# Layer 0's projected rows in DRAM: one copy of each part, repeated by the loads that read it

## The chip, the cores and the metric

The kernel runs on one core of one Trainium2 chip. A core has a tensor engine (PE, with its weight loads shown as PEld), a vector engine (DVE), a scalar engine (ACT), a general engine (POOL), a synchronisation engine (SP) that here only issues DMAs, and 16 DMA engines. The metric is the device time of one launch in microseconds. Three runs of the kernel before took 733.96, 735.86 and 736.60 us; the median, 735.86 us, is the time that is to be predicted anew. A change is told from no change here at about 0.5%, or 3.7 us.

## What is computed

Two transformer layers run over x of 8 batches x 256 tokens x 128 features. Each has a cross attention to a context of the same size, and a mixture of 8 experts of which every token uses two. The change touches only the attention of layer 0, which has 16 heads of width 8:

```python
q = _split_heads(query @ Wq.T + bq, B, Lq)
k = _split_heads(key @ Wk.T + bk, B, Lk)
scores = jnp.einsum('bhqd,bhkd->bhqk', q, k) / jnp.sqrt(jnp.float32(D_K))
mask = (hash_q[:, :, :, None] != hash_k[:, :, None, :]).astype(scores.dtype) * NEG
attn = jax.nn.softmax(scores + mask, axis=-1)
out = jnp.einsum('bhqk,bhkd->bhqd', attn, v)
```

## The kernel before

**Scores as one product of 74 or 77 rows.** A float32 product is had from bf16 matmuls: q and k are each cut into three bf16 parts whose sum is the float32 value, and all nine products of parts are summed by the tensor engine. So for each head both operands have 3 x 3 x 8 = 72 rows (`R_MASK`): for each of the nine pairs (i, j) and each of the 8 features d, the q operand `q9` holds part i of q and the k operand `k9` holds part j of k. The order of the 72 rows is free as long as both operands share it. Rows 72 and 73 carry the mask. Rows 74 to 76 (`R_MAX` to `R_ALL`) carry the negated row maxima, so that a second product gives score minus maximum, ready for the exponential.

**Stages.** The loop of layer 0 runs over n = 0 to 145. Step n is slot i = n % 16 of batch b = n // 16. In slot n the program has `scores` for slot n (line 533, two matmuls, then DVE's maximum on line 537), `probs` for the head of slot n - 15 (`LAG`; line 564, then ACT's exponential on line 571), and after every four heads `values0` (line 579). PE, ACT, DVE and SP run in the order in which the program was written out; SP's DMAs are therefore issued strictly one after another, and one that waits holds up those behind it.

**Side work.** Generators in the list `side` advance by one step in each slot, in the order in which they were appended. Two of them matter here:

- `prep0(b + 2)`, appended in slot i = 2 of batch b, makes q9 and k9 of batch b + 2, of which there are three buffers each. Counting its yields, its 14th and 15th steps (slots 15 of batch b and 0 of batch b + 1) issue the four mask rows (line 438), its 16th step falls into slot 1 of batch b + 1, and its 17th into slot 2. From step 16 on it writes the parts to a DRAM tile and loads them back: in steps 16 to 19 six writes (line 518), two, one, two and one to a step, and in step 20 the two reads (lines 521 and 522). `part` holds 128 partitions, which are (feature, head), by (part, q or k, token).
- `maxima(b, half)`, appended in slots 8 (half 0, heads 0 to 7) and 0 of the next batch (half 1, heads 8 to 15), has its third step in slots 10 and 2. That step transposes the maxima, copies them to `mT` (ACT, line 556) and issues one DMA of 12 KB on SP into rows 74 to 76 of q9 (line 557). The first `probs` that needs half 0 is in slot 15 of the batch, the first that needs half 1 in slot 7 of the next.

In slot 2 `prep0(b + 2)` stands before `maxima(b, 1)` in `side`, so its DMAs of that slot are ahead of that mT on SP's queue. Batch 0's operands are written without DRAM (`prep_first`). Batch 1's `prep0` is run to its end before the loop starts, with nothing between its steps.

**Other traffic.** POOL issues loads of later weights and inputs during batches 0 to 4, one in every second slot, and scatters rows to the experts during batches 5 to 7.

Of the kernel before, what the change touches and what calls it, by code (L numbers as in the profile page):

```python
# [12 lines left out]
BF16 = mybir.dt.bfloat16  # L13
# [6 lines left out]
S = 256  # L20
QT = S // P
D = 128
H = 16
DK0 = 8
# [27 lines left out]
NPART = 3  # L52
R_MASK = NPART * NPART * DK0
# [9 lines left out]
def kernel(  # L63
# [28 lines left out]
    nc = tc.nc  # L92
# [4 lines left out]
    dp = ctx.enter_context(tc.tile_pool(name="dp", bufs=3, space=bass.MemoryType.DRAM))  # L97
# [7 lines left out]
    def bank(tag, name, dt=F32):  # L105

        if tag == "any":
            third.append(third.pop(0))
            tag = third[-1]
        return ps.tile([P, 512 * 4 // mybir.dt.size(dt)], dt, tag=tag, name=name, bufs=1 if tag in ("pv", "y") else 2)  # L110
# [77 lines left out]
    with nc.allow_non_contiguous_dma(reason="two rows of biases, once"):  # L188
        for i, src in enumerate((bq0, bk0)):
            nc.scalar.dma_start(  # L190
                out=brow[:, i, :].rearrange("o (d g j) -> o d g j", d=DK0, g=4),
                in_=src.rearrange("(o j z) g -> o z g j", o=1, z=32)[:, :DK0],
# [190 lines left out]
    def norm_T(tiles, name, rows=None, lead=2):  # L383
        n = len(tiles)
        mv = sm.tile([P, GT, 2], F32, tag="mv", name=f"mv{name}", bufs=3)
        for i, t in enumerate(tiles):
            st = sm.tile([P, 6], F32, tag="bn", name=f"st{name}_{i}", bufs=3)
            nc.vector.bn_stats(out=st, in_=t)
            nc.vector.bn_aggr(out=mv[:, i, :], in_=st)
            if i == 1 and n > 2:  # L390
                yield
        ve = sm.tile([P, GT], F32, tag="ve", name=f"ve{name}", bufs=3)
        nc.vector.tensor_scalar(ve[:, :n], mv[:, :n, 1], EPS, None, ALU.add)
        rs = sm.tile([P, GT], F32, tag="rs", name=f"rs{name}", bufs=3)
        nc.gpsimd.tensor_tensor(rs[:, :n], ve[:, :n], mhalf[:, :n], ALU.pow)
        for _ in range(lead):
            yield
        xns = []
        for i, t in enumerate(tiles):
            if rows is None:  # L400
                xn = sm.tile([P, D], F32, tag="xn", name=f"xn{name}_{i}", bufs=4)
                to = xn
            else:
                xn = rows[:, i, 0, :D]
                to, t = rows[:, i, :, :D], t.unsqueeze(1).to_broadcast([P, 2, D])
            nc.vector.tensor_scalar(to, t, mv[:, i, 0:1], rs[:, i : i + 1], ALU.subtract, ALU.mult)
            xns.append(xn)
            if i == 1 and n > 2:
                yield
        for _ in range(1 if rows is None else 2):  # L410
            yield
        pt = bank("pt", f"np{name}")
        for i, xn in enumerate(xns):
            nc.tensor.transpose(pt[:, ts(i, P)], xn, ident)
        tag, bufs = (f"xnT{n}", 2) if rows is None else (f"xnTr{n}" if n == QT else f"xnT{n}", 1)
        xnT = wk.tile([P, n * P], F32, tag=tag, name=f"xnT{name}", bufs=bufs)
        nc.scalar.copy(xnT, pt[:, : n * P])
        yield
        return xnT
# [4 lines left out]
    def values(b):  # L424
        v = v0s[b % 4]
        pv = bank("pt", f"pvp0_{b}")
        for t in range(QT):
            nc.tensor.matmul(pv[:, ts(t, D)], lhsT=ct[b][:, ts(t, P)], rhs=wv0_sb, start=True, stop=True)
        nc.vector.tensor_tensor(
            v[:, :, :, :DK0],  # L430
            pv[:, : QT * D].rearrange("p (t h d) -> p t h d", t=QT, d=DK0),
            bv0_sb.rearrange("p (h d) -> p h d", d=DK0).unsqueeze(1).to_broadcast([P, QT, H, DK0]),
            ALU.add,
        )

    def mask_rows(b, t, k, engs):
        for i, eng in enumerate(engs):
            eng.dma_start(out=t[R_MASK + i : R_MASK + i + 1, :, :], in_=mrow[b * H : (b + 1) * H, k + i, :])
# [48 lines left out]
    def prep0(b):  # L487
        q9, k9, v = q9s[b % 3], k9s[b % 3], v0s[b % 4]
        xnT = yield from norm_T(xt[b * QT : (b + 1) * QT], f"a{b}", lead=6 if b >= 2 else 2)
        pq = bank("pt", f"pq0_{b}")  # L490
        nc.tensor.matmul(pq[:, :S], lhsT=wq0_sb, rhs=xnT, start=True, stop=True)
        nc.tensor.matmul(pq[:, S:], lhsT=wk0_sb, rhs=ct[b], start=True, stop=True)
        f = wk.tile([P, 2, S], F32, tag="g2", name=f"qk{b}", bufs=5)
        nc.scalar.activation(f[:, 0, :], pq[:, :S], AF.Identity, bias=bqk[:, 0:1], scale=1.0 / math.sqrt(DK0))
        nc.scalar.activation(f[:, 1, :], pq[:, S:], AF.Identity, bias=bqk[:, 1:2])
        yield

        part = wk.tile([P, NPART, 2, S], BF16, tag="pT", name=f"part{b}")
        rest = wk.tile([P, 2, S], F32, tag="g2", name=f"rest{b}", bufs=5)
        eng = nc.vector if b < 2 else nc.gpsimd  # L500
        eng.tensor_copy(part[:, 0], f)
        eng.tensor_tensor(rest, f, part[:, 0], ALU.subtract)
        eng.tensor_copy(part[:, 1], rest)
        eng.tensor_tensor(part[:, 2], rest, part[:, 1], ALU.subtract)
        yield
        values(b)
        yield
        for _ in range(2 if b >= 2 else 0):
            yield
        for t, k in ((q9, 0), (k9, 2)):  # L510
            mask_rows(b, t, k, (nc.sync, nc.sync))
            yield

        rows = dp.tile([2, R_MASK, H, S], BF16, tag="rows", name=f"rows{b}")
        for n, by in ((0, "(i j d) h s -> j (d h) i s"), (1, "(i j d) h s -> i (d h) j s")):
            to = rows[n].rearrange(by, i=NPART, j=NPART)
            for i in range(NPART):
                nc.sync.dma_start(out=to[i], in_=part[:, :, n, :])
                if b > 1 and i:
                    yield  # L520
        nc.sync.dma_start(out=q9[:R_MASK, :, :], in_=rows[0])
        nc.sync.dma_start(out=k9[:R_MASK, :, :], in_=rows[1])
        yield

    def scores(b, i):
# [579 lines left out]
    for _ in prep_first():  # L1105
        pass
    side.append(prep0(1))
    drain()
    for i in range(3):
# [4 lines left out]
    for n in range(NS * B + LAG + 3):  # L1114
        b, i = divmod(n, NS)
        if n < NS * B:
            scores(b, i)
        if 0 <= n - LAG < H * B:
            probs(*divmod(n - LAG, H))
        g, r = divmod(n - LAG - 5, 4)  # L1120
        if r == 0 and 0 <= g < 4 * B:
            values0(*divmod(g, 4))
            if g % 2:
                side.append(finish0(g // 4, g % 4 // 2))
        if i in (HH, 0) and HH <= n <= NS * B:
            side.append(maxima((n - 1) // NS, 1 if i == 0 else 0))
        if i == 2 and b + 2 < B:
            side.append(prep0(b + 2))
        if i == 6 and b in (3, 5, 7):
            one_by_one(route(0, 2 * (b - 3), GT, nc.gpsimd))  # L1130
            if b == 7:
                one_by_one(place(0, True))
                one_by_one(route(0, NT - 2 * QT, QT))
        if n == NS * B + 8:
            side.append(keys_values(0))
        tick()
        if n == NS * B + LAG - 2:
            begin0(range(4))
            tiles0 = run0()
        if n >= NS * B + LAG:  # L1140
            next(tiles0)
# [94 lines left out]
```

## Time and profile before

| | before |
|---|---|
| median of 3 runs | 735.86 us (733.96 to 736.60) |
| the profiled execution | 758.97 us, span 757.1 us |
| PE / DVE / ACT / POOL busy | 83% / 63% / 44% / 43% |
| mean granted PE clock | 0.927 of full speed |
| layer 0's attention in it | about 21 us (first `scores`) to 229 us (last `probs`) |
| DMA writes to the DRAM tile, line 518 | 42 of 192 KB, six for each of batches 1 to 7 |
| DMA reads of it, lines 521 and 522 | 7 + 7 of 576 KB |

The profile is of one execution, which took 3.1% longer than the median run. Its times are microseconds from the start of the span. A row of the timeline gives start, duration, engine and line, and in brackets how long the engine had been idle and what ended the idle time. An engine name with a q ("SPq") means the sequencer, which issues or waits; "[3.27 <-DMA x]" is a wait of 3.27 us that a DMA ended. "PEclk" is the share of full speed that the tensor engine's clock was granted.

### The profile page before, as it was taken

Reading aid. Unit: us, or ns where it says so; the run is one execution under the profiler, and the core shown is the slowest. Engines: PE = TensorE matmul, PEld = TensorE weight load, DVE = VectorE, ACT = ScalarE, POOL = GpSimd, SP = SyncE. Lnnn points to the kernel's source line nnn. Section 1 sums busy time; section 2 is a strip of 40 time slices with the busy share of each in tenths; the row PEclk is TensorE's granted clock in tenths of the full one; section 3 lists DMA queues with packets and bytes.
Section 4 is the critical chain, followed back from the end, with each engine's and each line's share of the span. In section 5 each row is a group of like instructions: output and inputs, shape, how many; then the busy total and the mean of one; then the engine's idle time right before and its main releaser. Section 6 shows DMA issues by size and latency. Waiting matters only on the chain.

```text
span 757.1 us, 15220 instructions
## 1 busy us (share of the span) xinstructions
PE 630.0 (83%) x4781; PEld 485.1 (64%) x4781; DVE 479.4 (63%) x1808; ACT 332.1 (44%) x1028; POOL 328.5 (43%) x398
## 2 busy tenths in 40 slices
PE   3699787768867779999999999999999784989990
PEld 2355454434435769986677777777777563879990
DVE  5778787666725455555777787877868772544442
ACT  1146554445522112235766565656556641423330
POOL 4445368260240544444433363535363551354442
PEclk9999998787768899999999999999999997999995
DMA  5577666650035446634020300000000015758845
GB/s 142 150 202 229 185 182 164 173 149 24 2 126 152 134 127 185 189 113 116 15 66 27 91 15 15 15 16 15 1 16 8 8 60 193 208 155 229 233 124 173
DMA packets 72318, 83.85 MB, mean 111 GB/s; under 512 B 9768, under 2 KB 55104, under 8 KB 71232
## 3 DMA queue, kind: packets, MB, share of 16 engines
q1 hardware_dynamic: 63640, 63.71, 30.2%
q0 software_dynamic: 7840, 18.97, 8.3%
q8 instruction: 39, 0.64, 0.4%
q14 instruction: 39, 0.32, 0.1%
q10 hardware_dynamic: 760, 0.21, 0.1%
HBM read 60.86 MB, written 30.60 MB: 121 GB/s over the span
## 4 chain that ended last, share of the span: by engine, by line
PE 27%; DVE 10%; issue 5%; ACT 4%; DMA 4%; POOL 4%; SPq 0%; POOLq 0%; ACTq 0%; DVEq 0%
PE s L962 4%; PE y L1037 4%; PE pt L1011 3%; PE o L1026 3%; POOL ys L860 3%; DVE ns L977 3%; PE pk L925 3%; ACT p L988 2%; PE pq L925 2%; DMA yy<-ys 2%; PE ph L830 2%; DVE pT L1013 2%; PE y L853 2%; DVE k L928 2%; PE pu L833 2%
## 5 line engine op out<-in xcount | busy, mean ns | idle before, releaser
L988 ACT ACTIVATE p<-ns,nm 128x256 f32<-128x256 f32 (+1 forms) x256 | 113.8, 447 | 33.9 <-DVE nm L977 29.2
L1001 POOL TENSOR_TENSOR p<-p,rd 128x1024 f32<-128x1024 f32 (+1 forms) x63 | 92.1, 1481 | 63.8 <-DVE rd L996 62.6
L860 POOL DMA_INDIRECT ys<-yj,xj x78 | 75.1, 963 | 89.5 <-DVE yj L858 78.3
L537 DVE TENSOR_REDUCE mx<-sc 128x2 f32<-128x512 f32 x128 | 83.8, 683 | 32.6 <-PE sc L533 25.2
L571 ACT ACTIVATE pT<-st 128x512 f32<-128x512 f32 x128 | 74.0, 596 | 64.2 <-PE st L564 60.7
L699 POOL DMA_INDIRECT xs<-rows,ati x64 | 63.0, 985 | 89.8 <-DVE rows L691 44.8
L977 DVE CUSTOM_DVE_ANT_0 ns<-s,tri 128x256 f32<-128x256 f32 (+1 forms) x256 | 77.0, 348 | 0.5 <-PE s L962 0.5
L1013 ACT COPY pT<-pt 128x512 f32<-128x512 f32 x64 | 36.8, 574 | 71.0 <-PE pt L1011 71.0
L564 PE MATMUL st<-q,k 77*128 77x256 bf16 x256 | 56.8, 310 | 13.2 <-DMA q<-mT 8.4
L533 PE MATMUL sc<-k,q 74*128 74x256 bf16 x256 | 57.2, 313 | 12.6 <-DVE mx L537 10.5
L1011 PE MATMUL pt<-ident,p 128*128 128x128 f32 x384 | 57.6, 278 | 4.9 <-POOL p L1001 3.2
L1011 PEld LDWEIGHTS pt<-ident,p 128*128 128x128 f32 x384 | 45.6, 142 | 24.3 <-DVE k L928 11.5
L1026 PE MATMUL o<-pT,v 128*64 128x256 f32 (+1 forms) x512 | 55.1, 339 | 4.9 <-ACT pT L1013 4.2
L839 DVE TENSOR_TENSOR h<-s,pu 128x256 f32<-128x256 f32 x78 | 24.0, 348 | 53.1 <-PE px L805 13.6
L823 ACT ACTIVATE h<-ph,wj 128x128 f32<-128x128 f32 x78 | 24.4, 364 | 72.7 <-issue 51.0
L820 PE MATMUL ph<-xT,wj 128*128 128x128 f32 x312 | 47.0, 296 | 9.9 <-DVE xT L807 5.7
L962 PE MATMUL s<-k,q 64*128 64x256 f32 (+1 forms) x512 | 53.2, 338 | 0.5 <-DVE nm L977 0.5
L1026 PEld LDWEIGHTS o<-pT,v 128*64 128x64 f32 x512 | 35.7, 138 | 23.7 <-ACT pT L1013 7.2
L962 PEld LDWEIGHTS s<-k,q 64*128 64x128 f32 x512 | 42.8, 186 | 10.3 <-issue 4.5
L988 ACT ACTIVATION_READ_ACCUMULATOR p<-ns,nm 128x1 f32 x256 | 48.6, 190 | 0.0
L820 PEld LDWEIGHTS ph<-xT,wj 128*128 128x128 f32 x312 | 40.2, 201 | 12.4 <-DVE xT L807 6.2
L533 PEld LDWEIGHTS <-q 74*128 74x128 bf16 x256 | 25.0, 109 | 35.9 <-issue 30.3
(227 smaller groups left out, 1290.5 us busy)
## 6 DMA issues: line engine op xcount, KB each, us to landing
wj<-wa SPq DMA_DIRECT2D x39, 352.0 KB
wj<-wa SPq DMA_DIRECT2D x39, 258.0 KB
rows<-part SPq DMA_DIRECT2D x42, 192.0 KB
xs<-blank SPq DMA_DIRECT2D x16, 325.0 KB
xj<-xs SPq DMA_DIRECT2D x78, 65.0 KB
yy<-ys SPq DMA_DIRECT2D x16, 256.0 KB
q<-rows SPq DMA_DIRECT2D x7, 576.0 KB
k<-rows SPq DMA_DIRECT2D x7, 576.0 KB
```

The costliest lines, as they stand in the source:

```text
L533: nc.tensor.matmul(sc[:, k, :], lhsT=q9s[b % 3][:R_MAX, h, ts(qt, P)], rhs=k9s[b % 3][:R_MAX, h, :], start=True, stop=True,)
L537: pace[0] = nc.vector.tensor_reduce(c0[b]["mx"][:, qt, 2 * u : 2 * u + 2], sc, AX.X, ALU.max)
L571: nc.scalar.activation(pT.rearrange("p t s -> p (t s)"), st, AF.Exp)
L699: nc.gpsimd.indirect_dma_start(out=xs[l][:, :], out_offset=to, in_=rows[:, i, k, :], in_offset=None),
L820: nc.tensor.matmul(phs[z][:, ts(i, P)], lhsT=wj[:, o : o + P], rhs=xT, start=True, stop=True)
L860: free(f"ys{l}", nc.gpsimd.indirect_dma_start(out=ys[l][:, :], out_offset=to, in_=yj, in_offset=None))
L962: nc.tensor.matmul(u["s"][a, r][:, (1 - qt) * S : (1 - qt) * S + n], lhsT=c1[b]["q"][rows, c, ts(qt, P)], rhs=c1[b]["k"][rows, c, :n], sta ...
L977: nc.vector.tensor_tensor_reduce(out=ns[:, o : o + n], in0=s[:, o : o + n], in1=tri[:, S - n :], scale=-1.0, scalar=3.0e38, op0=ALU.add, o ...
L988: nc.scalar.activation(p[:, o : o + n], ns[:, o : o + n], AF.Exp, bias=nm[:, a : a + 1], scale=-1.0, accum_out=u["sum"][:, 2 * i + a : 2 * ...
L1001: eng.tensor_tensor(p, p, rd[:, :, a : a + 1].to_broadcast([P, 4, n]), ALU.mult)
L1011: nc.tensor.transpose(pt[:, ts(n, P)], u["p"][:, i, (S, 0, P)[m] :][:, :P], ident)
L1026: nc.tensor.matmul(o[DK1 * r : DK1 * (r + 1), a, t * P :], lhsT=v[:, t, cols], rhs=pT, start=(t == 0), stop=True, skip_group_check=True,)
```

## The change

A part is written to DRAM once and not three times, and each read repeats a row three times. The 72 rows take a new order, r = 9d + 3i + j, the same that batch 0's operands have.

```diff
-        rows = dp.tile([2, R_MASK, H, S], BF16, tag="rows", name=f"rows{b}")
-        for n, by in ((0, "(i j d) h s -> j (d h) i s"), (1, "(i j d) h s -> i (d h) j s")):
-            to = rows[n].rearrange(by, i=NPART, j=NPART)
-            for i in range(NPART):
-                nc.sync.dma_start(out=to[i], in_=part[:, :, n, :])
-                if b > 1 and i:
-                    yield
-        nc.sync.dma_start(out=q9[:R_MASK, :, :], in_=rows[0])
-        nc.sync.dma_start(out=k9[:R_MASK, :, :], in_=rows[1])
+        rows = [dp.tile([R_MASK // NPART, H * S], BF16, tag=f"rows{n}", name=f"rows{b}_{n}") for n in range(2)]
+        to = rows[0].rearrange("(d i) (h s) -> i d h s", i=NPART, h=H)
+        for i in range(NPART):
+            nc.sync.dma_start(out=to[i], in_=part[:, i, 0, :])
+        nc.sync.dma_start(out=rows[1].rearrange("(j d) (h s) -> (d h) j s", j=NPART, h=H), in_=part[:, :, 1, :])
+        yield
+        src = rows[0].unsqueeze(1).to_broadcast([R_MASK // NPART, NPART, H * S])
+        nc.sync.dma_start(out=q9[:R_MASK, :, :], in_=src)
+        for j in range(NPART):
+            src = rows[1][ts(j, DK0), :].unsqueeze(1).to_broadcast([DK0, NPART, H * S])
+            nc.sync.dma_start(out=k9[j:R_MASK:NPART, :, :], in_=src)
         yield
```

The DRAM tile of q has 24 rows (d, i), that of k 24 rows (j, d), each of 8 KB. q's parts are written by three DMAs of 64 KB, k's by one of 192 KB. q9 is read by one DMA whose source has the counts 24, 3 and 4096; k9 by three whose sources have the counts 8, 3 and 4096, each into every third partition. The generator now writes in its 16th step, reads in its 17th, and is three steps shorter.

## Prediction

> **What bounds the kernel here.** I read the engine summary first, then the tensor engine's waits within layer 0's attention (20 to 230 us), then SP's and PE's timelines of one batch beside each other, then the windows around the waits.
>
> ```profile
> PE   3699787768867779999999999999999784989990
> PEclk9999998787768899999999999999999997999995
> ```
>
> PE is 60 to 90% busy through the attention, and its clock dips in some slices. It works in program order, so each wait of it moves the end. These are the waits:
>
> ```profile
> PE sc L533 <- DVE mx L537: 10.5, 16, 2.5
> PE st L564 <- DMA q<-mT: 8.4, 3, 4.3
> PE po L592 <- ACT oT L587: 8.3, 6, 6.6
> ...
> PE st L564 <- DMA k<-mrow: 3.3, 1, 3.3
> ```
>
> The reader should see that no large wait is for the row tile: q9 and k9 come in time (only 0.9 us, once). What PE waits for is mT, the 12 KB of maxima. SP's and PE's timelines of one batch show why:
>
> ```profile
> 59.47 1.21 SPq L438 DMA_DIRECT2D q<-mrow  x2
> 60.73 1.23 SPq L438 DMA_DIRECT2D k<-mrow  x2
> 62.00 1.98 SPq L518 DMA_DIRECT2D rows<-part  x3
> 64.63 0.79 SPq L557 DMA_DIRECT2D q<-mT  x1
> 65.46 1.57 SPq L518 DMA_DIRECT2D rows<-part  x3
> 67.28 0.36 SPq L521 DMA_DIRECT2D q<-rows  x1
> 69.79 0.31 SPq L522 DMA_DIRECT2D k<-rows  x1
> 73.61 0.77 SPq L557 DMA_DIRECT2D q<-mT  x1
> ```
>
> ```profile
> 67.92 0.39 PE L564 MATMUL st<-q,k 77*128 77x256 bf16 x2
> ...
> 76.43 0.38 PE L533 MATMUL sc<-k,q 74*128 74x256 bf16 x2 [0.23 <-DVE mx L537]
> 80.08 0.38 PE L564 MATMUL st<-q,k 77*128 77x256 bf16 x2 [3.27 <-DMA k<-mrow]
> ```
>
> The mT of 64.63 landed at 67.87 by the trace's semaphore records; the matmul at 67.92 is the first to need it. **It has no slack.** The mT of 73.61 was issued behind the two reads. It landed at 79.95, 6.3 us after its issue and 1.1 us after the read of k (78.86); later mTs with nothing beside them land in 2.0 us. The 3.27 us, which the view puts down to k<-mrow, are this wait. So on SP's queue a small DMA lands behind the large ones before it. And a wait costs more than itself:
>
> ```profile
> 80.00:84.00 4.00, 3.92 (x28) 0.58 0.69 209
> 125.00:135.00 10.00, 9.86 (x60) 0.50 0.56 136
> 141.00:145.00 4.00, 3.95 (x26) 0.50 0.74 202
> ```
>
> In these windows (length, PE busy, granted clock, DMA share, GB/s), right after the three mT waits, the clock is at half.
>
> **The change, part by part.**
>
> *Writes.* For each of seven batches 6 x 192 = 1152 KB become 3 x 64 + 192 = 384 KB. SP saves two issues (median 514 ns), but q's three writes have a destination counted by 8; the nearest row is the first batch's q<-part on SP, also 8 by 64 KB, 612 to 671 ns an issue and 2.2 us to land when quiet. Four writes take 3 x 0.62 + 0.52 = 2.4 us of SP, against 3.5 before. No engine waits for these bytes, and SP mostly waits itself: I take 0 (between -0.5 us a batch, were SP bound, and 0).
>
> *Reads.* The bytes stay 576 + 576 KB in 72 + 72 packets of 8 KB. SP issues four for two: +2 x 0.31 us. In a stretch with the reads nearly alone on the DMA engines (146 to 153 us) their queue keeps 68.5% of 16 engines busy at 169 GB/s, which fits twelve engines at work; a packet takes about 0.5 us. Twelve divides 72. Here the Trainium skill speaks against the change: "DMA: Bandwidth & Descriptors" ("Why a DMA increments its semaphore by 16 and not by 1", and the row "Use all 16 engines" of "Rules for kernel authors") says that a DMA uses the largest number of engines up to 16 that divides the outermost counts of both sides, the lowest-numbered ones. q's 72 and 24 still give 12. k's 24 and 8 give 8. An engine among the first eight then has 6 + 9 = 15 packets, not 6 + 6 = 12. By the row alone (twelve as now) the rings need 12 x 0.5 = 6.0 us, by the rule 15 x 0.5 = 7.5 us. I take the rule: the semaphore records of the trace give 12 arrivals to the reads now, 8 to q<-part and 3 to mT, which all fit it. So mT sits on rings 0 to 2, behind all 15.
>
> *Order.* This decides. Today the slot-2 mT is issued between the third and the fourth write, and the reads come three slots later. After the change the reads move into slot 2, and `prep0` stands before `maxima` in `side`: SP issues masks, four writes, **q's read, three reads of k, then mT**. The read of q waits for q's writes to land, the reads of k for k's; this wait exists today (SP waits 7.7 us in all before the read of k, up to 2.2 us at a time) but has nothing urgent behind it. Now mT is behind it, and PE behind mT.
>
> With T = the issue of the first write (62.00 in the rows above):
> - q's last write is issued at T + 1.25 and lands about 3.0 us later (the writes there take 2.9 to 3.4): q's read goes out at T + 4.3. k's write lands at T + 5.1, k's reads go out by T + 6.0, mT at T + 6.0 (before: T + 2.6).
> - q's first packet runs 1.1 us after the issue (as at 67.28); 15 packets of 0.5 us and some POOL loads among them make 7.5 us; mT lands 1.0 us behind: T + 13.9. Bounds: 15 packets at the shortest 0.31 us and quiet writes, T + 9.8; at 0.65 us, T + 16.4.
> - Needed at (slot 7, or where it would be without today's waits) T + 7.8, 5.9, 6.0, 7.5, about 6, and 8.6 in batches 1 to 6 (T = 41.72, 62.00, 78.74, 103.60, 134.85, 155.49). Stalls: 6.1 + 8.0 + 7.9 + 6.4 + 7.9 + 5.3 = **41.6 us**. With the bounds: 17 and 57.
>
> *What goes away.* The slot-10 mT finds the reads done, as they ran eight slots earlier. The waits for it in batches 2 and 4 go (3.3 + 3.3, with the small ones of that slot 7.3), in batch 5 the 0.75 us for mT and 0.87 for k<-rows. The 4.3 us of slot 7 in batch 5 are replaced by the new stall, which I reckoned from the unwaiting position: with slot overhead 4.7. Together **-13.6 us**. The next in line there are waits for DVE of 0.2 to 1 us.
>
> *Clock.* Half-clock stretches after the three large waits are 3.4, 10.2 and 6.8 us long, mean 6.8. PE-bound work loses half of a stretch, 3.4 us. The Trainium skill ("TensorE: Matmul & The Clock Gate", Part 1) reckons one window of 3.4 us until the clock is back, so 1.7 us a wait. Six waits for three: +3 x 3.4 = 10 by the rows, +3 x 1.7 = 5 by the rule. I take 5, since DVE, 90% busy in batch 3, hides part of a slower PE.
>
> *Start.* Batch 1's writes and reads stand in the opening chain, but PE has other scores to do until 40 us and the data land at 36: 0 (between -1 and +1).
>
> **Sum:** 41.6 - 13.6 + 5 = +33 us. Some of it is absorbed where PE already waits for ACT (6.6 us in batch 6): I take +30. The profiled execution of 759 would become 789; the median of 735.9 becomes **766 us**.
>
> **Rivals.**
> 1. *Forecast: mT behind the reads,* 766 us, from 745 to 792 by the bounds. Chance 0.70.
> 2. *Faster.* The slot-10 waits go (13.6 us and with them half of 24 us of half clock, some 10 us), and the reads run so fast, with a third of the write traffic, that mT keeps its time: about 726 us. It needs mT at T + 7 or so. From its lower bound of T + 9.8 this is 3 us away, so the packets would have to be faster than any in this trace, or the row rereads cheap. At the bound itself the sum is 17 - 14 - 5, about -2. Chance 0.11 for faster, 0.06 for within 0.5%.
> 3. *Heavier.* The three reads of k interleave in partitions; were each held until the one before it had landed, two more round trips of some 4.5 us (3 packets and 2 to 3 us of latency) would stand before mT: 6 x 9 = +54, about 820 us. Against it: the first batch's writes into every ninth partition are issued before one another's landing. Chance 0.07.
> 4. *Small loss,* packets near 0.35 us: +5 to +10, about 743 us. Chance 0.06.
> 5. *That the reads stay three slots later,* held by something I overlooked: then only traffic changes, and it is the "same" of rival 2.
>
> **Chances.** Slower 0.70 + 0.07 + 0.06 = 0.83, same 0.06, faster 0.11; 0.5% is what this measurement can tell from no change. The range, 740 to 792, leaves out the heavy case, and most of the faster one.
>
> **What would show it.** In SP's timeline mT of slot 2 comes after the reads, some 6 us after the first write. In PE's waits st <- DMA q<-mT grows from 8.4 us in 3 waits to about 40 in 6, one each in slot 7; those of slot 15 are gone; PEclk dips six times between 48 and 180 us. The write queue loses 7 x 768 KB. I am wrong if mT lands before slot 7, if the waits are in slot 0 for k<-rows, or if the clock holds through them.

## The result, and the profile after

The changed kernel takes 775.59 us in the median (772.79 to 776.73, 4 runs) against 735.81 us for the kernel before: **39.8 us slower, ratio 1.0538 (95% interval 1.0494 to 1.0583)**. The forecast was 766 us. Ratios, here and below, leave out executions more than 1.5% above the fastest of the same kernel; medians are of all.

First what should have become better. The DMA queue table of the changed kernel's page (packets, MB, share of 16 engines' time), whose row for SP's queue read 63640 packets and 63.71 MB before:

```profile
q1 hardware_dynamic: 52580, 58.20, 26.1%
```

The 7 x 768 KB are gone (5.5 MB), and the DMA engines are less busy. Now the engine summary and PE's waits within layer 0's attention, the same views that the prediction began with:

```profile
PE   3659549557788499999899999999999776689990
PEclk9658778767696779999999999999999998799995
```

```profile
PE st L566 <- DMA q<-mT: 47.8, 6, 9.7
PE sc L535 <- DVE mx L539: 14.6, 19, 2.6
PE po L594 <- ACT oT L589: 1.6, 6, 0.5
```

Six waits for mT, 47.8 us in all and up to 9.7 us each, stand where three waits of 8.4 us and a misnamed one of 3.3 us stood. In the clock row the second to sixth slices read 6, 5, 8, 7 and 7, where they all read 9 before. SP's and PE's timelines of one batch of the changed kernel (start, duration, engine and line) show how a wait comes about:

```profile
72.15 2.08 SPq L517 DMA_DIRECT2D rows<-part  x3
74.28 0.45 SPq L518 DMA_DIRECT2D rows<-part  x1
76.68 0.82 SPq L521 DMA_DIRECT2D q<-rows  x1
77.67 2.33 SPq L524 DMA_DIRECT2D k<-rows  x3
80.05 14.83 SPq L559 DMA_DIRECT2D q<-mT  x2
```

```profile
86.61 0.61 PE L566 MATMUL st<-q,k 77*128 77x256 bf16 x2 [9.70 <-DMA q<-mT]
```

The reader should see the order: writes, a pause of 2.0 us in which SP waits for them to land (74.73 to 76.68), four reads, and mT last, at 80.05 (the row merges it with the next one, issued at 94.13). It lands at 86.57 by the semaphore records, and PE goes on at 86.61. No wait for it is left in slot 15.

The two profiles differ by 16.7 us in their spans (757.1 and 773.8), and not by 39.8: the profiled execution of before was 23 us longer than its median. So the parts of the loss are read below from two profiles taken side by side on one chip.

### The profile page after: what moved, and what is told of

Read it like the earlier page. It is cut to its first block, busy times and chain, and to the rows that moved or that the text cites. A ratio compares the mean times of both kernels' runs of the same rounds, so it can differ in the third digit from the quotient of the medians.

```text
span 773.8 us, 15228 instructions
## 1 busy us (share of the span) xinstructions
PE 626.5 (81%) x4781; PEld 483.0 (62%) x4781; DVE 483.4 (62%) x1808; ACT 332.9 (43%) x1028; POOL 328.2 (42%) x398
## 4 chain that ended last, share of the span: by engine, by line
PE 23%; DVE 13%; issue 5%; ACT 4%; DMA 4%; POOL 4%; SPq 0%; POOLq 0%; DVEq 0%; ACTq 0%
PE y L1039 4%; PE s L964 4%; DVE ns L979 3%; POOL ys L862 3%; ACT p L990 3%; PE pk L927 3%; PE pt L1013 2%; PE o L1028 2%; DVE k L930 2%; DVE pT L1015 2%; DMA yy<-ys 2%; DMA xj<-xs 2%; PE y L855 2%; PE pq L927 2%; PE ph L832 2%
## 5 line engine op out<-in xcount | busy, mean ns | idle before, releaser
L566 PE MATMUL st<-q,k 77*128 77x256 bf16 x256 | 58.1, 316 | 48.9 <-DMA q<-mT 47.8
L535 PE MATMUL sc<-k,q 74*128 74x256 bf16 x256 | 57.7, 316 | 15.4 <-DVE mx L539 14.6
L566 PEld LDWEIGHTS <-k 77*128 77x128 bf16 x256 | 27.6, 111 | 60.4 <-DMA q<-mT 49.6
L1013 PEld LDWEIGHTS pt<-ident,p 128*128 128x128 f32 x384 | 46.3, 144 | 24.8 <-DVE k L930 10.8
L964 PEld LDWEIGHTS s<-k,q 64*128 64x128 f32 x512 | 42.8, 186 | 10.3 <-issue 4.5
L1028 PEld LDWEIGHTS o<-pT,v 128*64 128x64 f32 x512 | 33.9, 137 | 23.9 <-ACT pT L1015 6.8
```

The lines of the kernel that those rows point to most:

```text
L535: nc.tensor.matmul(sc[:, k, :], lhsT=q9s[b % 3][:R_MAX, h, ts(qt, P)], rhs=k9s[b % 3][:R_MAX, h, :], start=True, stop=True,)
L566: nc.tensor.matmul(st[:, ts(t, S)], lhsT=k9s[b % 3][:R_ALL, h, ts(t, P)], rhs=q9s[b % 3][:R_ALL, h, :], start=True, stop=True,)
L964: nc.tensor.matmul(u["s"][a, r][:, (1 - qt) * S : (1 - qt) * S + n], lhsT=c1[b]["q"][rows, c, ts(qt, P)], rhs=c1[b]["k"][rows, c, :n], sta ...
L1013: nc.tensor.transpose(pt[:, ts(n, P)], u["p"][:, i, (S, 0, P)[m] :][:, :P], ident)
L1028: nc.tensor.matmul(o[DK1 * r : DK1 * (r + 1), a, t * P :], lhsT=v[:, t, cols], rhs=pT, start=(t == 0), stop=True, skip_group_check=True,)
```

## The experiments

Beside every run stands the kernel before on the same chip. It took 759 to 761 us there, and 736 above; why is not known. So the ratio to the kernel before beside it is what counts. In the four expectations that name a time between 715 and 785 us, the microseconds were written for a before of 736 us (725 to 740 is a ratio of 0.985 to 1.005) and are read in that way.

**The pair again.** No edit: the changed kernel and the one before, profiled side by side.

> The changed kernel unaltered, timed and profiled beside the kernel before, because the two profiles at hand are of executions that differ in stages the change does not touch. Theory A (mT behind the reads, plus half clock after each wait): ratio to before 1.045 to 1.06, attention of layer 0 ends 35 to 45 us later than in the profile of before from the same chip, and the later stages are alike within 3 us.

> The kernel before, unaltered, for a profile from the same chip as the other runs of this call: waits for mT of 10 to 15 us in all, and the time of before's other runs within 1%.

The changed kernel took 795.87 us, before 760.02 us, ratio 1.0445 (1.037 to 1.0519), which is 34 us of 760. The profiled spans are 753.4 and 792.3 us. The stretch of PE's work from 40.6 us, after the opening, to the end of the attention, before and after (length, then busy time and instructions of PE, PEld, DVE, ACT and POOL, granted clock, DMA share, GB/s):

```profile
40.60:228.10 187.50, 147.68 (x1180) 85.79 (x1180) 124.32 (x365) 91.85 (x181) 83.70 (x132) 0.85 0.54 148
```

```profile
40.60:266.00 225.40, 155.63 (x1180) 90.42 (x1178) 127.25 (x365) 91.81 (x181) 83.80 (x132) 0.77 0.36 102
```

The stretch is 37.9 us longer, all of the 38.9 us between the spans but 1. PE does the same 1180 matmuls in 8.0 us more, at a mean clock of 0.77 and not 0.85, and is idle for 29.9 us more. Its waits for mT, before (the second row is misnamed, as in the first profile) and after:

```profile
PE st L564 <- DMA q<-mT: 11.4, 5, 4.7
PE st L564 <- DMA k<-mrow: 3.6, 1, 3.6
```

```profile
PE st L566 <- DMA q<-mT: 50.8, 6, 10.4
```

Of before's 15.0 us, 14.1 are in four waits over 0.7 us; so the large waits for mT grow by 36.7 us. The other waits over 0.7 us are 5.5 us shorter, the small ones 1.3 us. So 36.7 - 6.8 + 8.0 = 37.9: the stalls and the slower matmuls make the loss, and other waits give a little back. That the 8.0 us are the clock fits the records: of PE's busy time, 45.9 us fall into half clock before and 66.5 us after, and half of that growth is 10.3 us. Two of the stalls of the changed kernel in the columns of the stretch:

```profile
78.00:85.00 7.00, 0.00 (x0) 0.00 (x0) 0.00 (x0) 0.00 (x0) 0.00 (x0) 0.61 0.61 201
106.50:113.50 7.00, 0.00 (x0) 0.00 (x0) 0.00 (x0) 0.00 (x0) 1.03 (x1) 0.52 0.62 183
```

The engines stand still, but for 1.03 us of POOL, while the DMA engines move rows at 183 and 201 GB/s, with 12 KB behind them. The stall is in slot 7, and PE needs those rows in slot 0 of the next batch, nine slots later.

**The order alone.** The old 72-row tiles with the new timing:

```diff
-                if b > 1 and i:
-                    yield
+        yield
         nc.sync.dma_start(out=q9[:R_MASK, :, :], in_=rows[0])
```

> The kernel before with the new timing alone: 72 rows written three times over as before, all six writes in slot 1, the two reads in slot 2. Theory A: mT is behind the reads here too; two more writes make the wait before k's read 1 us longer, twelve packets and not fifteen in a ring make it 1.5 us shorter, so waits of 40 to 50 us in slot 7 and 765 to 785 us. Theory B: 730 to 740 us, since nothing is narrower than before.

800.28 us, ratio 1.0526 (1.0425 to 1.0627). Its waits of PE:

```profile
PE st L563 <- DMA q<-mT: 47.8, 5, 10.7
...
PE st L563 <- issue: 4.7, 1, 4.7
```

The second row is the sixth of these waits, in slot 7 of batch 6; the view names nothing for its end. Nothing is written once or read in a new pattern here, and the loss is whole. Theory B, that the narrower DMAs are to blame, falls.

**The reads back where they were.** The changed kernel with `for _ in range(3 if b > 1 else 0): yield` ahead of the reads.

> The changed kernel with its four reads held back by three steps, to slot 5, where the kernel before has them; writes and tiles as changed. Theory A (the slot-2 mT stands behind the reads on SP's queue and on the DMA rings): mT is issued before the reads again, the six waits of 47.8 us in slot 7 go, a few us come back in slot 15, and the time is 725 to 740 us. Theory B (the narrower DMAs, q's writes and k's reads, make the rows late whenever they are issued): still 760 us or more.

759.79 us, ratio 0.9982 (0.995 to 1.0013). PE's waits for mT shrink to this:

```profile
PE st L568 <- DMA q<-mT: 4.7, 2, 3.5
```

The new tiles and reads by themselves cost nothing that can be measured, and bring no more than 0.5%.

**One step later.** The same with a single `yield`, so that mT of slot 2 is issued just before the reads.

> The changed kernel with its reads one step later, in slot 3, just behind the mT of slot 2. Theory A: the mT of slot 2 goes out some 2.6 us after the first write and lands in time; the reads are over by slot 10, so the mT of that slot lands in time too: no wait for mT over 1 us, 715 to 732 us, below the kernel before. Theory B: 760 us or more.

758.22 us, ratio 0.9981 (0.9951 to 1.0011). One step takes away the whole loss. The gain that I expected on top of it (a ratio of 0.995 or less) is missing. PE's waits for mT have one of 8.5 us in them, and SP's timeline of this run says where it comes from:

```profile
PE st L568 <- DMA q<-mT: 10.7, 4, 8.5
```

```profile
125.30 1.01 SPq L278 DMA_DIRECT2D xs<-blank  x2
126.41 3.08 SPq L438 DMA_DIRECT2D q<-mrow  x2
...
134.61 0.81 SPq L561 DMA_DIRECT2D q<-mT  x1
```

In batch 5 SP issues nothing from 119.8 to 125.3: it stands at the DMAs of the blank rows, which POOL has not made yet. Masks, writes and mT come late behind them.

**mT on another queue.** `nc.scalar.dma_start` for mT, all else as changed.

> The changed kernel with mT's DMA issued by ACT, so on another queue, all else as changed. Theory A: mT waits neither for SP nor in SP's rings; it shares the DMA engines with the reads and lands in 2 to 4 us, the waits in slot 7 fall from 47.8 us to below 8 us, and the time is 720 to 740 us; 16 issues of about 0.7 us on ACT cost less than 5 us. If it is the load on the engines and not the order in a ring that holds mT up, the waits stay above 20 us and the time above 750 us. Theory B: 760 us or more.

769.32 us, ratio 1.0083 (1.0048 to 1.0119). The profile is of an execution of 762.35 us. PE's waits, and under them one of SP's own:

```profile
PE sc L535 <- DMA k<-mrow: 10.8, 1, 10.8
...
PE sc L535 <- DMA k<-rows: 5.6, 2, 5.4
...
PE st L566 <- DMA q<-mT: 4.2, 4, 2.3
```

```profile
SPq L524 <- DMA q<-mT: 24.9, 4, 11.9
```

Half a hit: the waits for mT go, the time is not reached. And the records do not show that the other queue lets mT pass the reads. SP and ACT in batch 4:

```profile
116.72 0.81 SPq L521 DMA_DIRECT2D q<-rows  x1
123.76 2.08 SPq L524 DMA_DIRECT2D k<-rows  x3
```

```profile
118.33 0.72 ACTq L559 DMA_DIRECT2D q<-mT  x1
```

By the semaphore records this mT landed at 123.70, 5.4 us after its issue, and the read of q that was in flight at 123.78. In batch 2 mT went out behind q's read in the same way and landed 2.4 us later, 0.9 us after that read. In the other four batches the reads were issued after mT. So no mT of slot 2 went out behind all four reads, as all six do in the changed kernel (5.8 to 9.4 us from issue to landing in its two profiles). Whether there mT waits for its turn in SP's queue, or for DMA engines that are busy with the reads, this run does not tell; it stays open.

The reads were held back by mT itself. A DMA on SP takes the semaphore of an earlier one: in all four waits of the row above, the read of k has the semaphore number of an mT, and SP stands until ACT has issued that mT and it has landed. The rows are then late for PE: the wait of 10.8 us, put down to k<-mrow, ends at 69.85, and k's last read landed at 69.71.

**The width of the reads.** Rows in the order r = 24i + 3d + j, so that all reads have the outer count 24:

```diff
+        nc.sync.dma_start(out=rows[0].rearrange("(i d) (h s) -> (d h) i s", i=NPART, h=H), in_=part[:, :, 0, :])
+        to = rows[1].rearrange("(d j) (h s) -> j d h s", j=NPART, h=H)
+        for j in range(NPART):
+            nc.sync.dma_start(out=to[j], in_=part[:, j, 1, :])
...
+        for i in range(NPART):
+            nc.sync.dma_start(out=k9[ts(i, R_MASK // NPART), :, :], in_=rows[1])
```

> The changed kernel with the rows in the order r = 24i + 3d + j, so that all reads have the outer count 24: q's part is one write of 192 KB, k's three of 64 KB, q9 is read once and k9 three times into 24 partitions next to one another. Writes still in slot 1, reads in slot 2. If the width of k's reads counts as the prediction had it (15 packets in the first rings and not 12): mT lands 1.5 us earlier, 9 us less than the changed kernel in all. If only the order counts: within 3 us of the changed kernel.

794.01 us, ratio 1.0445 (1.0391 to 1.0499), beside 795.87 us and 1.0445 (1.037 to 1.0519) for the changed kernel. The 9 us that the width was priced at would be 1.2% and lie outside these intervals; a difference of a few us does not. By the semaphore records k's reads run on twelve engines here and on eight in the changed kernel. By the packet records the 144 packets of 8 KB take 7.1 to 9.7 us here and 6.5 to 9.4 us there: in the later half of them, which is mostly k's, a packet takes 420 to 650 ns on the mean with twelve engines and 340 to 440 ns with eight. The total rate, 120 to 180 GB/s, is about the same in both.

**Blank rows from POOL.** Reads in slot 3, and the ten DMAs of the blank rows issued by POOL.

> The changed kernel with the reads in slot 3, and with the ten DMAs that write the blank rows issued by POOL, which makes those rows, and not by SP, where in the run with reads in slot 3 alone they held up masks, writes and mT of batch 5 (one wait of 8.5 us). Theory A: that wait goes as well, no wait for mT over 2 us, the time 8 to 15 us below the kernel before. If the batch-5 wait has another cause, it stays and the time is that of before.

761.55 us, ratio 1.0007 (0.9978 to 1.0037). A miss that PE's waits explain:

```profile
PE npa L414 <- DVE xna L406: 11.4, 4, 6.5
...
PE st L568 <- DMA q<-mT: 3.3, 3, 2.0
```

The waits for mT go as expected, but POOL, which then waits in its own order for its blank rows to land, is late with the norm of the next batch.

**Blank rows later.** Reads in slot 3, and 18 more steps ahead of the blank rows; and the same 18 steps in the kernel before.

> The changed kernel with the reads in slot 3 and the blank rows written 18 steps later, so that their DMAs are out of the way of batch 5's masks, writes and mT on SP, and POOL is left alone there too. Theory A (what is left of the waits for mT comes from SP being held up by the blank rows): no wait for mT over 2 us, time 6 to 15 us below the kernel before of the same chip. If the time is again that of before, waits for mT are no longer what sets it.

> The kernel before with the blank rows 18 steps later and nothing else: the wait of 4.4 us in slot 7 of batch 5 goes, those of slot 15 stay; 3 to 9 us below before. The difference to the other run of this call is what the single writes and the reads in slot 3 bring by themselves: 3 to 8 us.

With the reads in slot 3: 752.19 us against 759.27, **ratio 0.9895 (0.9856 to 0.9935)**, faster than both kernels. The kernel before with the steps alone: 760.68 us, 1.0019 (0.9986 to 1.0052), no gain. PE's waits for mT, of the first and then of the second:

```profile
PE st L570 <- DMA q<-mT: 5.8, 3, 2.7
```

```profile
PE st L566 <- DMA q<-mT: 13.6, 3, 7.6
...
PE st L566 <- DMA k<-mrow: 3.4, 1, 3.4
```

In the second the hold-up on SP moves on to batch 6: mT of slot 2 goes out behind blank rows and writes (a wait of 4.8 us), mT of slot 10 behind the last write, the reads and blank rows (7.6 us). The wait of slot 15 in batch 2 stays too; it is the row misnamed k<-mrow. In the first the reads are over before slot 10, and only 2.7 us is left of the longest wait. My expectation for the second, 3 to 9 us below before, was wrong, and that for the first, no wait over 2 us, was missed by a little. Neither the reads in slot 3 nor the later blank rows brought a gain alone; together they did. How much of it is due to the single writes was not tried apart.

## Why the prediction was right, point by point

- **Order.** Right, and shown: the order alone gives the loss with the old tiles, and one step's delay takes it away with the new ones. Whether it is the queue or the load that holds mT back behind the reads is open. mT was forecast at T + 13.9; the six of the changed kernel landed at T + 15.7, 14.4, 15.1, 15.0, 13.5 and 14.1, mean 14.6. That 0.7 us is 4 us over six batches.
- **Stalls.** Forecast 41.6 us, measured 47.8 and 50.8 in two profiles. The term that was too small is the landing of mT: q's read went out at T + 4.65 on the mean, not 4.3, and from there mT took 10.0 us, not 9.6. The other 2 us: PE came to slot 7 at T + 6.7 on the mean, 0.3 us sooner than forecast.
- **Reads and their width.** Wrong in its step. I priced k's reads at 15 packets of 0.5 us on each of the first eight DMA engines against 12, and took 9 us for that. In these runs a packet was shorter when fewer engines read, and the run with twelve engines everywhere was no faster. That the 7.5 us came out nearly right was luck: 144 packets at 157 GB/s, a rate in the middle of the measured ones, take as long. The issue of a read with a repeated source was mis-sized too: 0.64 to 0.69 us for k's (one of 0.79) and 0.81 to 0.84 for q's, not 0.31 (k's plain reads in the twelve-engine run take 0.32 to 0.41, one 0.88). mT is therefore issued at T + 7.8 on the mean, not T + 6.0. This cost little: in the twelve-engine run mT goes out 1.6 us sooner than in the changed kernel beside it, and PE goes on only 0.5 us sooner.
- **What goes away.** The waits in slot 15 went as forecast. Of before's 14.1 us for mT in the pair, 9.6 us were in slot 15 and none of that is left; the other 4.5 us, in slot 7 of batch 5, are replaced by the new stall. The sum had 13.6 us for both.
- **Clock.** Forecast +5 us, measured +8.0 us of PE time. In the changed kernel of the pair the half-clock stretches at the six stalls are 6.8 to 13.7 us long, but the first part of each falls into the stall itself. When PE goes on, 3.9 to 6.6 us are left, mean 5.2: between the one window of 3.4 us that the sum took and the 6.8 us of the rows that it set aside.
- **Absorbed.** I took 3 us off for work that hides the loss. The runs show none by name; the other waits that are 6.8 us shorter in the pair are single ones (6.4 and 5.3 us before against 6.0 after) that come and go between profiles.
- **Writes.** Zero, as forecast: with the reads back in slot 5 the saved 5.5 MB bring a ratio of 0.9982, with no change inside its interval.
- **Sums.** Three do not come out as written, and the 766 rests on none of them. The upper bound of 57 us of stalls leads to 784 us, not 792. The lower bound on mT's landing, with 2.2 us for a quiet write, is T + 10.2, not T + 9.8. The two gains of the faster rival lead to about 712 us, not 726.

So the mechanism held, and the stalls measured are 15 to 22% above the forecast of the main term. Put together for the profiled pair: the waits for mT come to 8.7 us more than the sum had (36.7 against 28.0), the clock to 3 us more, and other waits take off 3.8 us more than the 3 us for what is absorbed. That is the way from 30 to 37.9 us.

## What to carry to other kernels

When a transfer becomes cheaper or earlier, look at what stands behind it in its queue: here 1.2 MB of reads with fourteen slots to spare were put ahead of 12 KB that PE needed in five. Put the urgent small DMA first, by as little as one step, and only then count what the traffic saves. A stall of PE is to be priced with the slow clock after it, here about 8 us on top of 37.

## What was not expected

- The number of DMA engines of a read did not set its time: in the later half of the reads 8 KB packets took 340 to 440 ns with k's reads on eight engines and 420 to 650 ns with them on twelve, at about the same total rate.
- Moving mT to ACT's queue made SP wait 24.9 us for it ahead of k's reads through shared semaphores, so that the two queues were not independent.
- Profiles of executions near 760 us and the one of the changed kernel at 775 us differ in single waits outside the change. In the first profile of before the row below tells of two waits of ACT whose end the profile can't name; the changed kernel's first profile has none like it. After the attention that profile needs 517 us, where both profiles of before and the second of the changed kernel need 525 to 528. What causes this stays open.

```profile
ACT oT L587 <- remote: 11.8, 2, 6.6
```
